# Layer 1's gather table with padded rows and another order of columns

## The chip, the core and the metric

The kernel runs on one core of one Trainium2 chip. The metric is the device time of one execution in microseconds. Several executions are timed, and a profile is taken of one more. The engines named below are TensorE (PE; PEld is its weight load), VectorE (DVE), ScalarE (ACT), GpSimd (POOL) and the queue of SyncE (SP), which issues most transfers. Sixteen DMA engines move the data of all queues.

## The reference

A graph of N = 2708 nodes with 512 features goes through four layers. Each adds its result to its input and applies a layer norm. The adjacency matrix is sparse: about 0.15% of the entries off the diagonal are not zero, and the diagonal is kept.

```python
# layer 0
e1 = adj @ x
x = layernorm(x + (x - e1 * (diag + 1)) @ weight + bias)
# layer 1
type_sum = adj @ x
attn_a = sigmoid(concat(type_sum, x) @ Wa.T + ba);  attn_b = sigmoid(concat(type_sum, x) @ Wb.T + bb)
h = x @ W_sa
scores = (h @ a_left)[:, None] + (h @ a_right)[None, :]
e = where(adj != 0, exp(-leaky_relu(scores, 0.01)), 0)
x_a = (e / (sum(e, 1) + 1e-5)) @ h
x_b = adj @ (x @ W_gcnb) + b_gcnb
x = layernorm(x + sigmoid(attn_a * x_a + attn_b * x_b))
# layer 2: row-normalised incidence of adj times x;  layer 3: tanh(D^-1/2 (adj + I) D^-1/2 x @ W.T + b)
```

## The kernel before

The kernel treats the adjacency as a list of edges. A block is R = 113 destination rows, so there are NB = 24 blocks. Each block's edges off the diagonal are found on the chip in layer 0 and put in EC = 4 chunks of 128 slots; slots without an edge point past the table, and the gather leaves them out. A neighbour sum is then a product on TensorE: a 128 x 113 matrix per chunk, with the edge's value in the column of its destination, times 128 gathered rows. The program also holds a dense version, which does not run on these inputs.

**Layer 0** loads the adjacency block by block, finds the edges with VectorE, gathers rows of x, multiplies with three weight matrices and works in two kinds of pieces: blocks of 113 rows, and windows of 128 rows (`project0`, `residual0`, `norm0`, `next0`, `rest0`). For each window, `next0` and `rest0` compute h = x W_sa, x W_gcnb and four columns of scores and gates and collect them in one row of `st`, a tile from a ring of two. `store0` (L1051) writes that tile to `table[0]` in DRAM. A row before is 2D + 5 = 1029 columns: a one, 512 of h, 512 of x W_gcnb, the right score, the two gate columns, and another one. The first one, summed with the weights e, gives the sum of e; the last, summed with the adjacency values, gives the sum of a row.

**Layer 1** takes its blocks one after the other. `gather1` (L1371, through `gather`, L598) issues four indirect transfers from GpSimd, one per chunk, of whole table rows into one of three tiles `gath`, whose slots are WG = 1032 columns wide; column W1 of the tile, behind what is gathered, is filled with the inverse edge value (`values1`, L1374), so that a sum over it counts edges. `scores1` (L1387, its first instruction at L1390) makes the weights e from the gathered right score. `sums1` (L1402, matmuls at L1407) multiplies the adjacency values with the second half of the row: 256 columns, then 261. `scored_sums1` (L1412, matmuls at L1417) multiplies e with the first half: 257 columns, then 256. `gates1`, `gated1`, `both1`, `stats1` and `norm1` finish the block on VectorE, ScalarE and GpSimd and store it to `table[1]`. The diagonal's contribution doesn't come through the gather: `load_own1` (L634) loads the block's own table rows in order, columns 1 to 2D, to a place that `own_place` (L630) gives: two `shared` tiles and the first weight tile, two blocks in each. `move_rows` (L564) splits every transfer of 113 rows into 112 and 1.

Layers 2 and 3 gather rows of 512 columns from `table[1]` and `table[2]` into the same `gath` tiles, in the same slots.

The order of all instructions on each engine is written out by hand (`tc.manual_schedule()`, L647): engines take them in program order and wait on semaphores. In layer 1 the loop issues the gather of block i+2 while block i is summed, so the gather waits for the sums of block i−1, which read the same tile. On GpSimd the gather stands behind the two small instructions of `stats1` (L1480, L1481) of the block before. On VectorE `scores1` of the next block stands ahead of `stats1` of the last one.

Of the kernel before, what the change touches and what calls it, by code (L numbers as in the profile page):

```python
# [8 lines left out]
FP = mybir.dt.float32  # L9
AF = mybir.ActivationFunctionType  # L10
ALU = mybir.AluOpType
AX = mybir.AxisListType
P = 128
# [5 lines left out]
R = 113  # L19
# [428 lines left out]
def sparse_stack(  # L448
# [29 lines left out]
    nc = tc.nc  # L478
    N, D = x.shape
# [3 lines left out]
    NB = (N + R - 1) // R  # L483
    DB = D // P

    W1 = 2 * D + 5
    WG = 2 * D + 8

    const = ctx.enter_context(tc.tile_pool(name="const", bufs=1))
    dram = ctx.enter_context(tc.tile_pool(name="dram", bufs=1, space=bass.MemoryType.DRAM))  # L490
    big = ctx.enter_context(tc.tile_pool(name="big", bufs=1))
# [3 lines left out]
    def rows(i):  # L495
        return min(R, N - i * R)
# [4 lines left out]
    xr = xr_cols[:, :, :D]  # L501
    table = [dram.tile([N, W1 if k == 0 else D], FP, name=f"table{k}") for k in range(3)]
    deg_d = dram.tile([KB, P], FP, name="deg_d")
# [34 lines left out]
    def column(name, value):  # L538
        t = const.tile([P, NB], FP, name=name)
        nc.gpsimd.memset(t, value)  # L540
        return t

    row_cnt = const.tile([P, NB, 2], FP, name="row_cnt")
    nc.gpsimd.memset(row_cnt, 1.0)
    rowsum, cnt = row_cnt[:, :, 0], row_cnt[:, :, 1]
    adiag = column("adiag", 1.0)
# [17 lines left out]
    def move_rows(r, dst, src):  # L564

        c = r // 16 * 16
        for a, b in ((0, c), (c, r)):
            if a < b:
                nc.sync.dma_start(out=dst(a, b), in_=src(a, b))
# [10 lines left out]
    def times(o, uT, r, w, between=lambda: None):  # L580
        for f in range(DB):
            if f == DB // 2:
                between()
            nc.tensor.matmul(  # L584
                o, lhsT=uT[:, f, :r], rhs=w[:, f, :], start=(f == 0), stop=(f == DB - 1)
            )
# [11 lines left out]
    def gather(g, i, src, n):  # L598
        for c in range(EC):
            nc.gpsimd.indirect_dma_start(  # L600
                out=g[:, c, :n],
                out_offset=None,
                in_=src[:, :],
                in_offset=bass.IndirectOffsetOnAxis(ap=source[:, i, c : c + 1], axis=0),
                bounds_check=last,
                oob_is_err=False,
            )
        return g
# [11 lines left out]
    NGB = 3  # L620
    gath = [big.tile([P, EC, WG], FP, name=f"gath{k}") for k in range(NGB)]
    gflat = [g.rearrange("p c w -> p (c w)") for g in gath]


    shared = [big.tile([P, KB * R], FP, name=f"shared{k}") for k in range(2)]

    w0_sb = big.tile([P, DB, D], FP, name="w0_sb")
    NO = 6

    def own_place(i):  # L630
        t = (*shared, w0_sb.rearrange("p b d -> p (b d)"))[i % NO // 2]
        return t[:, i % 2 * 2 * D :][:, : 2 * D]

    def load_own1(i):  # L634
        r = rows(i)
        own1[i] = own_place(i)
        move_rows(
            r, lambda a, b: own1[i][a:b, :],
            lambda a, b: table[0][i * R + a : i * R + b, 1 : 2 * D + 1],
        )  # L640

    own1 = {}
# [5 lines left out]
    with ExitStack() as phase:  # L648
# [60 lines left out]
        def wrows(w):  # L709
            return min(P, N - w * P)  # L710
# [7 lines left out]
        def to_blocks(w):  # L718

            g, end = w * P, w * P + wrows(w)  # L720
            while g < end:
                i, q = g // R, g % R
                n = min(end, (i + 1) * R) - g
                move_rows(
                    n, lambda a, b: xr_cols[q + a : q + b, i, :],
                    lambda a, b: x1w[w % 2][g - w * P + a : g - w * P + b, :],
                )
                g += n
# [53 lines left out]
        totals = first.tile([P, NB], FP, name="totals")  # L782
        st_ring = [first.tile([P, W1], FP, name=f"st{k}") for k in range(2)]
        for t in st_ring:
            nc.gpsimd.memset(t[:, 0 : W1 : W1 - 1], 1.0)
        nojunk = first.tile([P, KB * R], mybir.dt.uint8, name="nojunk")


# [57 lines left out]
        def negatives(i):  # L846
            nc.scalar.activation(
                nojunk, abuf[i % NA].rearrange("p b i -> p (b i)"), AF.Relu, scale=-1.0,
                accum_out=negs[:, i : i + 1],
            )  # L850
# [175 lines left out]
        def next0(w):  # L1026

            r = wrows(w)
            xT = turned0["x", w]
            st = st_ring[w % 2]  # L1030
            half = (D + 6) // 2
            ends = (0, half, D)
            for k in range(2):
                o = ps_o.tile([P, D], FP, tag="o", name=f"h{k}_{w}")
                times(o[:r, :half], xT, r, w_sa_sb[:, :, k * half : (k + 1) * half])
                nc.scalar.copy(
                    st[:r, 1 + ends[k] : 1 + ends[k + 1]], o[:r, : ends[k + 1] - ends[k]]
                )
            col = o[:r, half - 6 : half]
            nc.scalar.copy(x1w[w % 2][:r, D:], col)  # L1040
            nc.scalar.copy(st[:r, 2 * D + 1 : 2 * D + 4], col[:, 1:4])
            to_blocks(w)
            st0[w] = st
# [112 lines left out]
        negatives(2)  # L1156
        for a, b in ((0, EC * D), (EC * D + 4 * D + 12, EC * WG)):
            nc.scalar.memzero(gflat[1][:, a:b])
# [148 lines left out]
    ediag = const.tile([P, NB], FP, name="ediag")  # L1307
# [20 lines left out]
    for g, (c0, _) in enumerate(SEGS):  # L1328
        at = slice(8 * g, 8 * g + 8)
# [12 lines left out]

    H = D // 2
    e_at = (slice(0, 1 + H), slice(1 + H, 1 + D))
    s_at = (slice(1 + D, 1 + D + H), slice(1 + D + H, W1 + 1))
    SR = 2 * D + 1

    def halves(t, r):  # L1350
        return t[:r, :].rearrange("p (k d) -> p k d", k=2)
# [3 lines left out]
    edge_s, edge_e, sum_s, sum_e, vb1, gate1, v1 = ({} for _ in range(7))  # L1355
# [15 lines left out]
    def gather1(i):  # L1371
        gather(gath[i % NGB], i, table[0], W1)

    def values1(i, chunks):  # L1374

        if i not in edge_s:
            edge_s[i] = spool.tile([P, EC, R], FP, tag="s", name=f"s1_{i}", bufs=3)
            nc.scalar.copy(gath[i % NGB][:, :, W1], inverse[:, i, :])
        for c in chunks:
# [32 lines left out]
    def scored_sums1(i):  # L1412
        g, e, r = gath[i % NGB], edge_e.pop(i), rows(i)
        sum_e[i] = ps_1e.tile([P, 2, D], FP, tag="e1", name=f"l1e{i}")
        for k, at in enumerate(e_at):
            for c in range(EC):
                nc.tensor.matmul(  # L1417
                    sum_e[i][:r, k, k : k + at.stop - at.start], lhsT=e[:, c, :r],
                    rhs=g[:, c, at], start=(c == 0), stop=(c == EC - 1),
                )  # L1420

    def gates1(i):

        r = rows(i)

        gate1[i] = small.tile([P, 2], FP, tag="gate", name=f"gate{i}")
        nc.vector.tensor_add(
            gate1[i][:r, :], sum_s[i][:r, 1, H + 1 : H + 3], gates[:r, i, :]
        )
        nc.scalar.activation(gate1[i][:r, :], gate1[i][:r, :], AF.Tanh, scale=0.5)  # L1430
        nc.scalar.copy(row_cnt[:r, i, :], sum_s[i][:r, 1, H + 3 : H + 5])

    def gated1(i):

        r = rows(i)
        vb = vb1[i] = spool.tile([P, D], FP, tag="vb", name=f"l1b{i}")
        nc.vector.scalar_tensor_tensor(  # L1437
            halves(vb, r), halves(own1[i][:, D:], r), adiag[:r, i : i + 1],
            sum_s.pop(i)[:r, :, :H], op0=ALU.mult, op1=ALU.add,
        )  # L1440
        nc.vector.tensor_add(vb[:r, :], vb[:r, :], bg_bc[:r, :])
        gate = gate1[i]
        nc.vector.tensor_scalar(
            gate[:r, :], gate[:r, :], 0.5, 0.5, op0=ALU.mult, op1=ALU.add
        )
        nc.scalar.activation(vb[:r, :], vb[:r, :], AF.Copy, scale=gate[:r, 1:2])

    def both1(i):

        r, agg = rows(i), sum_e.pop(i)  # L1450
        rec = small.tile([P, 1], FP, tag="rec", name=f"rec{i}")
        nc.vector.scalar_tensor_tensor(
            rec[:r, :], agg[:r, 0, 0:1], 1e-5, ediag[:r, i : i + 1], op0=ALU.add, op1=ALU.add
        )
        nc.vector.reciprocal(rec[:r, :], rec[:r, :])
        nc.vector.tensor_mul(rec[:r, :], rec[:r, :], gate1.pop(i)[:r, 0:1])
        va = work.tile([P, D], FP, tag="u", name=f"l1a{i}")
        nc.vector.scalar_tensor_tensor(
            halves(va, r), halves(own1.pop(i)[:, :D], r), ediag[:r, i : i + 1],
            agg[:r, :, 1 : H + 1], op0=ALU.mult, op1=ALU.add,  # L1460
        )
        v = work.tile([P, D], FP, tag="v", name=f"l1v{i}")
        nc.vector.scalar_tensor_tensor(
            v[:r, :], va[:r, :], rec[:r, :], vb1.pop(i)[:r, :], op0=ALU.mult, op1=ALU.add
        )

        nc.scalar.activation(v[:r, :], v[:r, :], AF.Tanh, scale=0.5)
        v1[i] = v
# [126 lines left out]
    for i in range(NB):  # L1595
# [3 lines left out]
        if i > 0:  # L1599
            both1(i - 1)  # L1600
# [272 lines left out]
```

## Time and profile before

| | |
|---|---|
| runs, median (lowest to highest) of 3 | 988.39 us (983.14 to 991.57) |
| profiled execution | 972.5 us |
| its span, first to last instruction | 970.3 us |
| granted TensorE clock, mean | 0.967 |
| bytes moved by DMA | 201.69 MB in 133516 packets, mean 208 GB/s |
| packets under 512 B | 82457 |
| gathers from the tables | 288 issues; issue to landing 3.1, 4.4, 9.6 us (least, median, most) |
| stages in the span | layer 0 to about 410 us, layer 1 to about 625, layer 2 to about 773, layer 3 to the end |

In the lines of the profile an instruction is named by its line in the source, its engine, and output <- inputs, with buffer numbers left out. `gath<-table,source` is a gather from any of the tables; `shared<-table` and `w_sb<-table` are own rows. An idle time is put down to the instruction whose end released it. A table of stretches gives each engine's busy time, then the granted clock, the mean busy share of the 16 DMA engines, and the rate at which they moved data.

### The profile page before, as it was taken

The page shows a single profiled execution, that of the slowest core. Times are in us where ns is not written, and L with a number is a line of the kernel's source. Part 1 is how long each engine was busy: PE and PEld are TensorE (multiplying, and loading weights), DVE is VectorE, ACT ScalarE, POOL GpSimd, SP SyncE. Part 2 cuts the span into 40 slices and gives each one's busy share as a digit, 9 for nine tenths or more (in the row PEclk, how much of TensorE's full clock was granted, in tenths as well). Part 3 has the DMA queues.
Part 4 walks back from the last instruction along what each step waited for, and adds up shares of the span by engine and source line. Part 5 has one row for each costly group of instructions (what it writes and reads, how often), then busy time and mean ns, then how long its engine had stood idle before and what let it go on. Part 6 is the DMA issues. An engine that isn't in the chain of part 4 may idle for free.

```text
span 970.3 us, 11188 instructions
## 1 busy us (share of the span) xinstructions
PE 890.4 (92%) x2957; PEld 492.3 (51%) x2957; DVE 686.6 (71%) x1807; ACT 528.0 (54%) x1221; POOL 466.6 (48%) x536
## 2 busy tenths in 40 slices
PE   6789999999999999988898899888898989999994
PEld 2446556556565555456676677533333334444441
DVE  7787899878898853068887879777777526556543
ACT  5676667867677753357776777434455312222222
POOL 3223232423133220066666667367777478767640
PEclk8889999999999999989999999999999999999998
DMA  9987786987888444388999998257777556655531
GB/s 242 317 206 199 209 244 185 281 221 220 215 234 236 138 133 144 110 283 274 299 297 310 305 299 279 97 161 220 215 227 213 142 164 182 177 155 173 163 108 32
DMA packets 133516, 201.69 MB, mean 208 GB/s; under 512 B 82457, under 2 KB 82503, under 8 KB 133446
## 3 DMA queue, kind: packets, MB, share of 16 engines
q0 software_dynamic: 36864, 111.73, 39.1%
q1 hardware_dynamic: 96581, 89.18, 32.1%
q8 instruction: 25, 0.41, 0.2%
q14 instruction: 46, 0.37, 0.1%
HBM read 181.83 MB, written 27.80 MB: 216 GB/s over the span
## 4 chain that ended last, share of the span: by engine, by line
PE 58%; DMA 19%; DVE 8%; issue 5%; POOL 5%; SPq 2%; ACT 2%; POOLq 0%; DVEq 0%; ACTq 0%
DMA gath<-table,source 16%; PE o_l L584 15%; PE l3a L613 9%; PE hb L584 7%; PE h L584 7%; PE l0a L613 6%; POOL gath L600 4%; PE l2a L613 3%; PE l1s L1407 2%; PE fetched L915 2%; PE unread L1537 2%; SPq L677 2%; DMA gath<-in_x_dram 1%; PE l1e L1417 1%; PE tr_l L1066 1%
## 5 line engine op out<-in xcount | busy, mean ns | idle before, releaser
L600 POOL DMA_INDIRECT gath<-table,source x288 | 314.4, 1092 | 158.2 <-issue 62.8
L600 POOL DMA_INDIRECT gath<-in_x_dram,source x96 | 97.2, 1013 | 224.8 <-issue 189.4
L1407 PE MATMUL l1s<-gath,s 128*113 128x256 f32 (+3 forms) x384 | 98.3, 412 | 21.1 <-DVE l1b L1437 20.6
L613 PE MATMUL l2a<-gath,s_left 128*113 128x512 f32 (+1 forms) x192 | 96.8, 619 | 16.4 <-DMA gath<-table,source 16.2
L1407 PEld LDWEIGHTS l1s<-gath,s 128*113 128x113 f32 (+1 forms) x384 | 71.5, 191 | 48.2 <-DVE l1b L1437 28.1
L613 PE MATMUL l3a<-gath,s 128*113 128x512 f32 (+1 forms) x192 | 88.3, 602 | 3.1 <-DMA gath<-table,source 3.1
L613 PE MATMUL l0a<-gath,s 128*113 128x512 f32 (+1 forms) x192 | 87.3, 595 | 0.5 <-DMA gath<-in_x_dram,source 0.5
L584 PE MATMUL o_l<-shared,uT_l 128*113 128x512 f32 (+1 forms) x192 | 86.5, 593 | 0.7 <-ACT uT_l L577 0.7
L1417 PE MATMUL l1e<-gath,e 128*113 128x257 f32 (+3 forms) x384 | 87.0, 379 | 0.0
L584 PE MATMUL hb<-w_gc_sb,uT_x 128*128 128x512 f32 (+1 forms) x176 | 83.3, 601 | 0.0
L584 PE MATMUL o_l<-w_sb,uw 128*128 128x512 f32 (+1 forms) x176 | 81.4, 606 | 0.2
L584 PE MATMUL h<-w_sa_sb,uT_x 128*128 128x259 f32 (+1 forms) x352 | 80.8, 382 | 0.0
L1417 PEld LDWEIGHTS l1e<-gath,e 128*113 128x113 f32 (+1 forms) x384 | 68.0, 177 | 15.3 <-DVE e L1400 0.2
L584 PEld LDWEIGHTS h<-w_sa_sb,uT_x 128*128 128x128 f32 (+1 forms) x352 | 64.8, 185 | 19.8 <-issue 6.1
L1792 ACT ACTIVATE y<-l3v,mv_l 113x512 f32<-113x512 f32 (+1 forms) x24 | 19.5, 813 | 87.4 <-DVE mv_l L1788 80.6
L613 PEld LDWEIGHTS l2a<-gath,s_left 128*113 128x113 f32 (+1 forms) x192 | 29.6, 179 | 73.1 <-DMA gath<-table,source 56.2
L584 PEld LDWEIGHTS o_l<-shared,uT_l 128*113 128x113 f32 (+1 forms) x192 | 33.9, 178 | 48.9 <-issue 47.3
L613 PEld LDWEIGHTS l0a<-gath,s 128*113 128x113 f32 (+1 forms) x192 | 33.3, 177 | 41.1 <-issue 36.2
L613 PEld LDWEIGHTS l3a<-gath,s 128*113 128x113 f32 (+1 forms) x192 | 32.6, 180 | 41.6 <-issue 38.3
L1294 DVE TENSOR_SCALAR s<-niota_r,nrow,edges 128x113 f32<-128x113 f32 x192 | 51.4, 345 | 0.0
L1766 DVE SCALAR_TENSOR_TENSOR l3v<-o_l,d_inv,b_bc 113x512 f32<-113x512 f32 (+1 forms) x25 | 18.1, 728 | 46.8 <-PE o_l L584 46.7
L862 DVE FIND_INDEX8 where_all<-rec_all,shared 128x8 uint32<-128x678 f32 (+1 forms) x64 | 51.2, 800 | 0.0
(244 smaller groups left out, 1573.9 us busy)
## 6 DMA issues: line engine op xcount, KB each, us to landing
shared<-in_adj_dram SPq DMA_DIRECT2D x14, 1186.5 KB
table<-st SPq DMA_DIRECT2D x21, 514.5 KB
gath<-in_adj_dram SPq DMA_DIRECT2D x7, 1186.5 KB
shared<-table SPq DMA_DIRECT2D x16, 448.0 KB
gath<-in_x_dram SPq DMA_DIRECT2D x21, 256.0 KB
xi<-in_x_dram SPq DMA_DIRECT2D x23, 224.0 KB
table<-xr SPq DMA_DIRECT2D x23, 224.0 KB
table<-y SPq DMA_DIRECT2D x23, 224.0 KB
```

The source lines that it names most:

```text
L584: nc.tensor.matmul(o, lhsT=uT[:, f, :r], rhs=w[:, f, :], start=(f == 0), stop=(f == DB - 1))
L600: nc.gpsimd.indirect_dma_start(out=g[:, c, :n], out_offset=None, in_=src[:, :], in_offset=bass.IndirectOffsetOnAxis(ap=source[:, i, c : c ...
L613: nc.tensor.matmul(agg[:r, :], lhsT=s[:, c, :r], rhs=g[:, c, off : off + D], start=(c == 0), stop=(c == EC - 1),)
L677: nc.sync.dma_start(out=a[:TAIL, NF, :r], in_=adjT[NF * P :, at])
L862: nc.vector.max_index(out=where_all[:, i, g * 8 : (g + 1) * 8], in_max=top, in_values=seg)
L915: nc.tensor.matmul(t["fetched"][:, c, : 3 * NS], lhsT=t["q"][:, c * P : (c + 1) * P], rhs=rec_all[:, i].rearrange("p k s -> p (k s)"), sta ...
L1294: nc.vector.tensor_scalar(s[:, c, :], niota_r, nrow[:, i, c : c + 1], edges[:, i, c, 1:2], op0=ALU.is_equal, op1=ALU.mult,)
L1407: nc.tensor.matmul(sum_s[i][:r, k, : at.stop - at.start], lhsT=s[:, c, :r], rhs=g[:, c, at], start=(c == 0), stop=(c == EC - 1),)
L1417: nc.tensor.matmul(sum_e[i][:r, k, k : k + at.stop - at.start], lhsT=e[:, c, :r], rhs=g[:, c, at], start=(c == 0), stop=(c == EC - 1),)
L1537: nc.tensor.matmul(o[:, :cols], lhsT=ident, rhs=bg_bc[:, :cols], start=True, stop=True)
L1766: nc.vector.scalar_tensor_tensor(v[:r, at], o[:r, at], d_inv[:r, i : i + 1], b3_bc[:r, at], op0=ALU.mult, op1=ALU.add,)
L1792: nc.scalar.activation(y[:r, :], v[:r, :], AF.Identity, bias=mv[:r, 3:4], scale=mv[:r, 2:3])
```

## The change

Table rows become W1 = 1040 columns, 2D + 5 rounded up to 16, with zeros in the 11 columns added. A slot of `gath` becomes W1 + 4 = 1044 columns. The one for the sum of e moves from the start of the row to the place behind h, so that h starts the row and x W_gcnb, the scores, the gates and the last one keep their columns. Own rows are loaded as the first 1025 columns, from the start of the row, and take 1025 columns in their places; the first weight tile grows by two columns for it. The matmuls of `scored_sums1` take 256 and then 257 columns; the second half in `sums1` runs on to the inverse edge values behind the padding, so it takes 272 columns where it took 261. `gates1` picks the row sum and the count out of it with a step of 12. The transfers, and the order of instructions, stay as they are; one more memset per `st` tile is added. (What the diff writes as a new width and order of columns is all of it; layer 0's order of work is the same in both kernels.)

```diff
-    W1 = 2 * D + 5
-    WG = 2 * D + 8
+    W1 = (2 * D + 5 + 15) // 16 * 16
+    WG = W1 + 4
...
-    w0_sb = big.tile([P, DB, D], FP, name="w0_sb")
+    w0_own = big.tile([P, 4 * D + 2], FP, name="w0_sb")
+    w0_sb = w0_own[:, : DB * D].rearrange("p (b d) -> p b d", d=D)
     NO = 6
 
     def own_place(i):
-        t = (*shared, w0_sb.rearrange("p b d -> p (b d)"))[i % NO // 2]
-        return t[:, i % 2 * 2 * D :][:, : 2 * D]
+        t = (*shared, w0_own)[i % NO // 2]
+        return t[:, i % 2 * (2 * D + 1) :][:, : 2 * D + 1]
 
     def load_own1(i):
...
-            lambda a, b: table[0][i * R + a : i * R + b, 1 : 2 * D + 1],
+            lambda a, b: table[0][i * R + a : i * R + b, : 2 * D + 1],
...
         for t in st_ring:
-            nc.gpsimd.memset(t[:, 0 : W1 : W1 - 1], 1.0)
+            nc.gpsimd.memset(t[:, 2 * D + 5 :], 0.0)
+            nc.gpsimd.memset(t[:, D : 2 * D + 5 : D + 4], 1.0)
...
                 nc.scalar.copy(
-                    st[:r, 1 + ends[k] : 1 + ends[k + 1]], o[:r, : ends[k + 1] - ends[k]]
+                    st[:r, ends[k] : ends[k + 1]], o[:r, : ends[k + 1] - ends[k]]
                 )
...
-    e_at = (slice(0, 1 + H), slice(1 + H, 1 + D))
+    e_at = (slice(0, H), slice(H, 1 + D))
     s_at = (slice(1 + D, 1 + D + H), slice(1 + D + H, W1 + 1))
...
-                    sum_e[i][:r, k, k : k + at.stop - at.start], lhsT=e[:, c, :r],
+                    sum_e[i][:r, k, : at.stop - at.start], lhsT=e[:, c, :r],
...
-        nc.scalar.copy(row_cnt[:r, i, :], sum_s[i][:r, 1, H + 3 : H + 5])
+        nc.scalar.copy(row_cnt[:r, i, :], sum_s[i][:r, 1, H + 3 : H + 4 + W1 - 2 * D - 4 : W1 - 2 * D - 4])
...
-            halves(vb, r), halves(own1[i][:, D:], r), adiag[:r, i : i + 1],
+            halves(vb, r), halves(own1[i][:, D + 1 :], r), adiag[:r, i : i + 1],
...
-            rec[:r, :], agg[:r, 0, 0:1], 1e-5, ediag[:r, i : i + 1], op0=ALU.add, op1=ALU.add
+            rec[:r, :], agg[:r, 1, H : H + 1], 1e-5, ediag[:r, i : i + 1], op0=ALU.add, op1=ALU.add
...
-            agg[:r, :, 1 : H + 1], op0=ALU.mult, op1=ALU.add,
+            agg[:r, :, :H], op0=ALU.mult, op1=ALU.add,
```

## The prediction

> **What bounds the kernel now.** I read the page first, for the engines and the chain of work that ended last.
>
> ```profile
> span 970.3 us, 11188 instructions
> PE 890.4 (92%) x2957; PEld 492.3 (51%) x2957; DVE 686.6 (71%) x1807; ACT 528.0 (54%) x1221; POOL 466.6 (48%) x536
> ...
> PE 58%; DMA 19%; DVE 8%; issue 5%; POOL 5%; SPq 2%; ACT 2%; POOLq 0%; DVEq 0%; ACTq 0%
> DMA gath<-table,source 16%; PE o_l L584 15%; PE l3a L613 9%; PE hb L584 7%; PE h L584 7%; PE l0a L613 6%; POOL gath L600 4%; PE l2a L613 3%; PE l1s L1407 2%; PE fetched L915 2%; PE unread L1537 2%; SPq L677 2%; DMA gath<-in_x_dram 1%; PE l1e L1417 1%; PE tr_l L1066 1%
> ```
>
> TensorE carries most of the chain, but its largest single term is a transfer: gathers from the tables, 16% of the span. The changed table feeds layer 1 (about 423 to 616 us), so next come busy times by stretch. Columns: PE, PEld, DVE, ACT, POOL busy us, granted clock, DMA share, GB/s.
>
> ```profile
> 423.00:440.00 17.00, 15.01 (x62) 10.88 (x61) 10.89 (x25) 9.02 (x26) 10.44 (x12) 0.93 0.92 326
> 440.00:585.00 145.00, 128.10 (x544) 99.66 (x544) 119.74 (x306) 101.95 (x255) 94.97 (x102) 0.95 0.96 299
> 589.00:616.00 27.00, 25.24 (x114) 19.43 (x112) 24.43 (x62) 19.38 (x49) 16.05 (x18) 1.00 0.67 228
> 640.00:770.00 130.00, 115.26 (x262) 41.91 (x262) 95.60 (x263) 62.43 (x115) 95.60 (x93) 0.99 0.73 209
> 785.00:950.00 165.00, 164.17 (x454) 72.27 (x455) 90.51 (x217) 42.11 (x67) 111.06 (x133) 1.00 0.55 157
> ```
>
> From 440 to 585 us the DMA engines are 96% busy; nothing else is. From 589 us the last gathers are in and PE is 93% busy. Which wait ends last shows in VectorE's order of time, at its first instruction on a gathered block (`scores1`, L1390):
>
> ```profile
> 503.24 0.63 DVE L1390 TENSOR_TENSOR e<-gath,s_left 128x452 f32<-128x452 f32 x1
> 512.61 0.63 DVE L1390 TENSOR_TENSOR e<-gath,s_left 128x452 f32<-128x452 f32 x1 [1.66 <-DMA gath<-table,source]
> ...
> 596.87 0.62 DVE L1390 TENSOR_TENSOR e<-gath,s_left 128x452 f32<-128x452 f32 x1
> 604.49 0.62 DVE L1390 TENSOR_TENSOR e<-gath,s_left 128x452 f32<-128x452 f32 x1
> ```
>
> Without a wait a block takes 7.62 us (604.49 − 596.87); while gathers run, blocks take 7.6 and 9.4 us in turn, and the long one has a wait on the gather. Between 435.92 and 589.25 us, 18 blocks take 8.52 us each. So a perfect DMA could return at most 18 × (8.52 − 7.62) = 16.2 us here; the waits named DMA sum to 14.4 us (1.32, 0.87, 1.42, 0.48, 1.38, 1.66, 1.91, 1.43, 0.33, 2.04, 1.35, 0.22).
>
> [...] The trace can test this on the adjacency loads, whose pieces are unaligned at both ends:
>
> ```profile
> DMA packets 7936, 3.52 MB, mean 282 GB/s; under 512 B 7936, under 2 KB 7936, under 8 KB 7936
> ```
>
> That is 2.5 to 15 us: 12.5 us × 16 engines / 7936 = 25.2 ns a piece. [...] what the trace shows of speed is the 25.2 ns above, with pieces that land off any 32 B grid.
>
> **The change part by part.** The order of instructions on every engine is unchanged except for two more memsets on GpSimd; no DMA is moved past another, no wait is added.
>
> *Gather source, 4116 B at pitch 4116 to 4160 B at pitch 4160 (64 B aligned).* About 452 rows per block. [...] By bytes it is a loss: 44 × 452 = 19.9 KB per block at 299 GB/s = 0.067 us, × 18 blocks = 1.2 us if all of it is on the path. I take the middle of 0 and 1.2: **+0.6 us**. [...] The adjacency loads bound it: [...] misalignment, and all else, is at most about 9 ns a piece. Per block each engine handles 28 gathered rows and 7 own rows; 35 × 9 ns × 18 = 5.7 us. Gain between 0 and 5.7 us; value taken 0[...].
>
> *Own rows, 4096 B from 4 B past a row start to 4100 B from the start.* [...] nothing, and counted in the 35 above. The 113th row goes alone: [...] taken as 0.
>
> *Gather destination.* Compiled addresses: all slots of `gath` began on a 32 B boundary at pitch 4128; at pitch 4176 slots 1 and 3 begin 16 B past one. [...] Bound from both sides: no gain, because no slot gets a better start; cost at most the same 9 ns on half the rows: 14 per engine and block × 9 ns × 18 = 2.3 us in layer 1, and in layer 2 (22 blocks, about 0.6 on the path, as PE is 89% busy there) 1.7 us; layer 3 is hidden by PE, busy 164.17 of 165 us. Taken 0, range 0 to 4.
>
> *Matmuls.* The shape rows of TensorE:
>
> ```profile
> L1407 PE MATMUL l1s<-gath,s 128*113 128x256 f32 x184 | 51.3, 425 | 20.8 <-DVE l1b L1437 20.4 <-POOL mv_l L1481 0.3
> L1407 PE MATMUL l1s<-gath,s 128*113 128x261 f32 x184 | 47.2, 402 | 0.0
> ```
>
> The 261 columns become 272. A block's 16 passes of `l1s` take 3.74 us for 8 × 517 = 4136 columns, 0.90 ns each; 88 more are 0.08 us. Until 585 us the waits on gathers hide this (cover gone: 20 × 0.08 = 1.6 us). In the last four blocks it is on the path: **+0.3 us**. `l1e` swaps 257+256 for 256+257: nothing.
>
> *Nothing, with cover.* Stores of the table: 44 × 2708 B = 119 KB, 0.4 us at 299 GB/s, spread over layer 0, where DMA is 67 to 78% busy and PE 252 of 255 us. Memsets of 11 columns: about 0.2 us at 3.8 us, covered by GpSimd's 0.73 us of waiting for the adjacency. ACT's clears: 3 × 48 more elements at 0.9 ns = 0.13 us; the first lies in a 2.15 us wait, the others could show 0.1 us. The strided `row_cnt` copy still moves two elements.
>
> **Sum:** +0.6 + 0.3 = +0.9 us on the profiled execution, 972.5 (span 970.3 plus 2.2 around it) to 973.4. The median of the runs is 988.39, 1.6% above that execution; I carry the 0.9 over: **989.3 us**. Its own range, from the bounds: −5.7 + 0.3 to +1.2 + 1.6 + 4.0 + 0.8 (clears, memsets, stores uncovered), 983 to 996.
>
> **Rivals.** *Faster: [...]* Random 4 KB rows are not adjacency pieces; if each misaligned read also costs memory time, 35 rows × t × 18 blocks = 630 t. From t = 16 ns the gain passes 1%; that is 8% of the 0.21 us an engine spends per row (26.00 MB on the gather queue in 70.4% of 16 engines' time from 440 to 560 us). It saturates when the DMA waits are gone: −14.4 + 1.5 of matmul then uncovered, about −13; halfway between threshold and end: 977 us. For: DMA is at 96%, and 299 GB/s is below the best slices of 423 to 440 us. Against: those slices reach 428 GB/s with the same unaligned rows.
>
> *Slower: half of all gathered rows now land off the 32 B grid.* Place: layers 1 and 2. Price: 14 rows per engine and block × t × (18 + 13) = 434 t; beyond t = 23 ns it costs 10 us and decides; at 28 ns, 12 us and **1000 us**. For: before, every row started on the grid. Against: the adjacency pieces land off it at 25 ns in all.
>
> *It does not do what it says:* DMA limits layer 1 through the number of rows and the two gathers in flight[...]; then only TensorE's 0.3 us remain: 988.7, inside the forecast.
>
> **Numbers.** Forecast 0.55, faster 0.27, slower 0.18. A difference of 1% (about 10 us) is about what a measurement of this kernel can tell from no change. The range 977 to 999 leaves out about half of each rival, 2 in 10.
>
> **What would show it.** Packets under 512 B fall by 24 × 16 = 384 to about 82070; moved bytes rise to 202.3 MB; `l1s` shows 128x272; L1390 keeps its alternation of 7.6 and 9.4 us and its 14 us of waits. Rate per engine in the gathers of 440 to 585 us rising by over 8%, and the waits vanishing, would be the first rival; longer waits of `l2a` on gathers in layer 2 would be the second. What I would have most wrong is a memory cost that 452 B pieces don't show.

## The result, and the profile after

Twelve executions of each kernel give 986.02 us in the median for the changed kernel (981.04 to 991.32) and 990.14 us for the one before (983.14 to 992.35). The recorded ratio is 0.9982, with a 95% interval of 0.996 to 1.0004: no difference. (The quotient of the two medians is lower, 0.9958; in a later series, below, it is 0.9996, with a recorded ratio of 0.9993.) The prediction was 989.3 us, "no change".

The profiled execution of the changed kernel seems to say otherwise: 985.9 us, span 984.2, where the profile before had a span of 970.3. So this section asks two things: whether the predicted terms are there, and what the 14 us between the two profiles are. First the page of the kernel after: its span, its engines, its DMA packets, and the chain of work that ended last by engine.

```profile
span 984.2 us, 11190 instructions
PE 891.9 (91%) x2957; PEld 495.6 (50%) x2957; DVE 686.6 (70%) x1807; ACT 527.7 (54%) x1221; POOL 468.8 (48%) x538
...
DMA packets 133515, 202.29 MB, mean 206 GB/s; under 512 B 82456, under 2 KB 82502, under 8 KB 133445
...
PE 64%; DMA 12%; DVE 7%; issue 5%; POOL 4%; ACT 2%; another core or an unknown queue 2%; SPq 2%; POOLq 0%; DVEq 0%; ACTq 0%
```

The two added instructions are there (POOL x538, before x536), and so is the padding: 202.29 MB, before 201.69. Packets under 512 B are 82456 where they were 82457; the prediction wanted 384 fewer. The busy times of the engines are those of before within 3.3 us. New in the chain is "another core or an unknown queue", 2%: the chain stands at an instruction that waited for something the profile cannot name.

Next the busy times by stretch of the kernel after; the columns are those of the table before (PE, PEld, DVE, ACT, POOL busy us, granted clock, DMA share, GB/s).

```profile
440.00:585.00 145.00, 125.10 (x546) 96.24 (x545) 120.22 (x307) 102.43 (x255) 96.96 (x104) 0.99 0.97 305
...
640.00:770.00 130.00, 108.26 (x244) 42.49 (x244) 87.17 (x236) 55.77 (x106) 94.99 (x90) 0.93 0.69 200
785.00:950.00 165.00, 158.72 (x424) 69.15 (x425) 84.56 (x206) 39.14 (x62) 114.39 (x134) 0.97 0.56 161
```

Layer 1 (440 to 585 us) is as before: DMA 97% busy (96%), 305 GB/s (299). Layers 2 and 3 are where PE does less in the same time: 108.26 of 130 us where it was 115.26, and 158.72 of 165 where it was 164.17. GpSimd, which issues the gathers, is busy for 94.99 us in the first (before 95.60) and 114.39 in the second (before 111.06).

VectorE's order of time in layer 1, at the first instruction of `scores1` (now L1394), shows the same alternation and the same kind of wait:

```profile
432.29 0.62 DVE L1394 TENSOR_TENSOR e<-gath,s_left 128x452 f32<-128x452 f32 x1
...
534.59 0.63 DVE L1394 TENSOR_TENSOR e<-gath,s_left 128x452 f32<-128x452 f32 x1 [1.75 <-DMA gath<-table,source]
542.33 0.63 DVE L1394 TENSOR_TENSOR e<-gath,s_left 128x452 f32<-128x452 f32 x1
551.99 0.63 DVE L1394 TENSOR_TENSOR e<-gath,s_left 128x452 f32<-128x452 f32 x1 [1.95 <-DMA gath<-table,source]
...
585.47 0.63 DVE L1394 TENSOR_TENSOR e<-gath,s_left 128x452 f32<-128x452 f32 x1 [0.46 <-DMA gath<-table,source]
600.95 0.62 DVE L1394 TENSOR_TENSOR e<-gath,s_left 128x452 f32<-128x452 f32 x1
608.53 0.62 DVE L1394 TENSOR_TENSOR e<-gath,s_left 128x452 f32<-128x452 f32 x1
```

Blocks 7.7 and 9.7 us apart (542.33 − 534.59, 551.99 − 542.33), the long one ending with a wait on a gather; 18 blocks from 432.29 to 585.47 us, so 153.18 us, where it was 153.33; waits at this line of 14.16 us in all, 12.47 of them put down to the gathers and one of 1.69 to nothing that the profile names; before, 14.4 were put down to the gathers. The last starts, without gathers to wait for, are 7.63 and 7.58 us apart; before, the same two distances are 7.62 and 7.59.

The chain of the kernel after, in order of time, from layer 2 on: start, length, what it was spent on.

```profile
668.38 5.93 another core or an unknown queue
...
704.91 2.44 another core or an unknown queue
...
731.91 5.67 another core or an unknown queue
...
766.47 2.92 another core or an unknown queue
...
805.66 4.97 another core or an unknown queue
```

These are 21.9 us, and the profile before has none. The account of the two spans: layer 0 ends earlier (the first instruction of `scores1` starts at 420.94 us, before 424.54: −3.6), the 18 blocks −0.15, layer 2 from the first to the last of its 24 normalisations (`l2v<-l2a` on VectorE) 134.6 us where it was 123.7: +10.9, and what is then missing of +13.9, with the 4.97 us at 805.66 in it, +6.8. The experiments must tell whether these waits belong to the change.

### The profile page after: what moved, and what is told of

Its sections match the earlier page's. It is cut to its first block, busy times and chain, and to the rows that moved or that the text cites. A ratio compares the mean times of both kernels' runs of the same rounds, so it can differ in the third digit from the quotient of the medians.

```text
span 984.2 us, 11190 instructions
## 1 busy us (share of the span) xinstructions
PE 891.9 (91%) x2957; PEld 495.6 (50%) x2957; DVE 686.6 (70%) x1807; ACT 527.7 (54%) x1221; POOL 468.8 (48%) x538
## 2 busy tenths in 40 slices
DMA packets 133515, 202.29 MB, mean 206 GB/s; under 512 B 82456, under 2 KB 82502, under 8 KB 133445
## 4 chain that ended last, share of the span: by engine, by line
PE 64%; DMA 12%; DVE 7%; issue 5%; POOL 4%; ACT 2%; another core or an unknown queue 2%; SPq 2%; POOLq 0%; DVEq 0%; ACTq 0%
PE o_l L585 15%; DMA gath<-table,source 9%; PE l3a L614 9%; PE l2a L614 8%; PE hb L585 8%; PE h L585 7%; PE l0a L614 7%; POOL gath L601 3%; PE unread L1541 2%; PE fetched L918 2%; SPq L679 1%; PE l1s L1411 1%; PE tr_l L576 1%; PE tr_l L1069 1%
## 5 line engine op out<-in xcount | busy, mean ns | idle before, releaser
L1411 PE MATMUL l1s<-gath,s 128*113 128x256 f32 (+3 forms) x384 | 95.9, 404 | 22.2 <-DVE l1b L1441 21.9
L1411 PEld LDWEIGHTS l1s<-gath,s 128*113 128x113 f32 (+1 forms) x384 | 68.8, 184 | 49.6 <-DVE l1b L1441 30.2
L614 PE MATMUL l3a<-gath,s 128*113 128x512 f32 (+1 forms) x192 | 90.5, 616 | 2.8 <-DMA gath<-table,source 2.8
L1421 PE MATMUL l1e<-gath,e 128*113 128x256 f32 (+3 forms) x384 | 87.0, 379 | 0.0
L1421 PEld LDWEIGHTS l1e<-gath,e 128*113 128x113 f32 (+1 forms) x384 | 68.2, 178 | 15.4
L1541 PE MATMUL unread<-bg_bc,ident 128*128 128x512 f32 x80 | 44.2, 669 | 21.3 <-remote 17.1
L614 PEld LDWEIGHTS l2a<-gath,s_left 128*113 128x113 f32 (+1 forms) x192 | 33.9, 190 | 57.5 <-issue 38.7
```

The lines of the kernel that those rows point to most:

```text
L614: nc.tensor.matmul(agg[:r, :], lhsT=s[:, c, :r], rhs=g[:, c, off : off + D], start=(c == 0), stop=(c == EC - 1),)
L1411: nc.tensor.matmul(sum_s[i][:r, k, : at.stop - at.start], lhsT=s[:, c, :r], rhs=g[:, c, at], start=(c == 0), stop=(c == EC - 1),)
L1421: nc.tensor.matmul(sum_e[i][:r, k, : at.stop - at.start], lhsT=e[:, c, :r], rhs=g[:, c, at], start=(c == 0), stop=(c == EC - 1),)
L1541: nc.tensor.matmul(o[:, :cols], lhsT=ident, rhs=bg_bc[:, :cols], start=True, stop=True)
```

## The experiments

The theory is that of the prediction: layer 1's blocks wait for DMA throughput, the padding costs little more than its bytes, and alignment decides nothing. Against it stand three rivals: the start of an unaligned source row costs time of its own, 16 ns a row or more (the faster one, theory B below); destinations off the 32 B grid cost time (the slower one); and gathers limited by the number of rows and by having two blocks under way, not by the bytes that they move (theory C). The measure is the stretch of 18 blocks in layer 1, from the third to the twenty-first start of `scores1`'s first instruction, read in each profile; the whole time goes by medians, against runs of the kernel before on the same chip. There were three series: the first without own rows, the wide pitch and one size of slots; the second the wide pitch again, the order of columns alone, and the kernel before; the third the changed kernel and both sizes of slots.

### Layer 1 without its own rows

```diff
         own1[i] = own_place(i)
-        move_rows(
-            r, lambda a, b: own1[i][a:b, :],
-            lambda a, b: table[0][i * R + a : i * R + b, 1 : 2 * D + 1],
-        )
```

This is the kernel before, without layer 1's own-row loads, a fifth of what it moves per block (113 of about 565 rows); the gathers, their number and their order stay. The diagonal's part of layer 1 is computed from whatever lies in those tiles.

> The kernel before, with the loads of own rows in layer 1 left out (the diagonal's part of layer 1 is then computed from stale data; every other instruction stays). Measure: the 18 blocks of layer 1 between the third and the twenty-first start of scores1, 153.3 us in the kernel before. Theory A, layer 1 waits on what 16 DMA engines can move: per block 0.46 of 2.55 MB go, 8.52 x 0.82 = 7.0 us is below the 7.62 us that a block takes without waits, so the stretch falls to 137 to 140 us, the waits of scores1 on gathers to under 3 us, and the whole kernel is 13 to 16 us faster. Theory C, layer 1 waits on the latency of two gathers in flight and not on throughput: the stretch falls by less than 5 us.

Measured: 972.35 us against 990.05, ratio 0.983 (0.9785 to 0.9876). VectorE's order of time in this kernel, the same instruction (here L1386), and the stretch of 440 to 585 us:

```profile
503.57 0.62 DVE L1386 TENSOR_TENSOR e<-gath,s_left 128x452 f32<-128x452 f32 x1
511.19 0.62 DVE L1386 TENSOR_TENSOR e<-gath,s_left 128x452 f32<-128x452 f32 x1
518.81 0.62 DVE L1386 TENSOR_TENSOR e<-gath,s_left 128x452 f32<-128x452 f32 x1
526.47 0.63 DVE L1386 TENSOR_TENSOR e<-gath,s_left 128x452 f32<-128x452 f32 x1
```

```profile
440.00:585.00 145.00, 136.51 (x608) 105.97 (x608) 132.46 (x341) 113.22 (x286) 111.47 (x114) 1.00 0.84 278
```

Every block takes 7.6 us, no start has a wait, and PE does 136.51 us of work in the 145 where it did 128.10. The 18 blocks take 137.91 us instead of 153.33: 15.4 of the at most 16.2 us that the prediction read off. So layer 1 waits for what the DMA engines carry in all, and having only two gathers under way, which is so here too, doesn't hold it back: that half of the third rival falls. The other half, rows against bytes, isn't decided by this run, which takes both away; the next section has more on it.

The same run answers for the 113th row. The page's packets:

```profile
DMA packets 130386, 190.58 MB, mean 197 GB/s; under 512 B 82036, under 2 KB 82082, under 8 KB 130317
```

The copy of the kernel before (run below) has 133445 packets under 8 KB and 82456 under 512 B. So the own rows of 24 blocks were 133445 − 130317 = 3128 packets, of which 82456 − 82036 = 420 are small. The other 2708 are exactly one packet a row, the single rows too. In the packet records of the two traces the 2708 are all the packets of 4096 B on that queue, and the 420 are 4 B each. That the small ones go with the transfers is read from their number alone: it fits 16 beside 112 rows, 1 beside a single row, and 16 and 13 beside the last block's 109 rows, which are split into 96 and 13: 23 × (16 + 1) + 16 + 13 = 420. A store of 113 rows in layer 2 of the kernel after has the same count, 113 packets of 2048 B and 17 of 4 B from 694 to 696 us. A single row of 4096 B travels whole, as one packet.

### Where rows start: a wide pitch, from and off a 256 B boundary

The changed kernel with rows of 4352 B (17 × 256), 59 unused columns ahead of the data that are gathered too. In one kernel every row starts at a 256 B boundary, counted from the start of the table; in the other, every row starts 252 B past one, with the same bytes gathered to the same places. (A constant of layer 3 lies in another tile, to make room.) The stores and own rows leave the unused columns out and start off the boundary in both, 236 and 232 B past one. The core of the edit (S = 0 or 63; the offset of the gather is in the second kernel alone):

```diff
-    W1 = (2 * D + 5 + 15) // 16 * 16
+    K, S = 59, 0
+    W1 = K + 2 * D + 5
...
+    rows1 = table[0].rearrange("n w -> (n w)")[S : S + N * W1].rearrange("(n w) -> n w", w=W1)
...
                 in_offset=bass.IndirectOffsetOnAxis(ap=source[:, i, c : c + 1], axis=0),
+                element_offset=off,
...
-        gather(gath[i % NGB], i, table[0], W1)
+        gather(gath[i % NGB], i, table[0], W1, S)
...
-    e_at = (slice(0, H), slice(H, 1 + D))
+    e_at = (slice(K, K + H), slice(K + H, K + 1 + D))
```

The unused columns are zeroed at the start of layer 0, in pieces of 236 B; these pieces, too, start on or off the boundary.

> The changed kernel with a pitch of 1088 columns (4352 B, a multiple of 256 B), all 1088 gathered, 59 unused columns ahead of the data, so that every gathered row starts on a 256 B boundary: [...] 192 B more. The third bias row moves to a shared tile to make room, and the unused columns are zeroed early in layer 0, which may cost a few us there; the layer-1 stretch (153.2 us in the changed kernel) is what counts. [...] A by bytes: 192 x 452 B at 299 GB/s x 18 = +5.2 us, 158 us. Theory B, [...] the stretch is below 153 us in spite of the bytes. Theory C: 153 us.

> The same as the run before it, but every gathered row starts 252 B past a 256 B boundary (63 columns further on; same bytes, same rows, same places in the tiles): [...] This is the cost of an unaligned start by itself. [...] Theory B: at least 16 ns a row, +8 us or more. By bytes, and by theory C: no difference (under 1 us).

Measured: 999.77 us, ratio 1.0095 (1.0063 to 1.0127), from the boundary; 1001.57 us, ratio 1.0126 (1.0098 to 1.0154), from 252 B past it. Both were run again on another chip:

> The wide rows that start on a 256 B boundary once more, for a second profile. The first had 157.9 us in the layer-1 stretch, 4.7 over the changed kernel, as the bytes alone would have it (158); but the same rows started 252 B past the boundary had 154.0. If the 3.9 us between them are of the start: 157.5 to 158.5 again. If they are spread of one profile against another: anywhere between 154 and 158.

> The wide rows started 252 B past a boundary once more. [...] if they cost nothing, the two agree within the spread; if rows on a boundary are slower for another reason, 154 again against 158.

Measured: 983.89 us, ratio 1.0117 (1.0077 to 1.0157), and 987.3 us, ratio 1.0153 (1.0109 to 1.0198). The 18 blocks of the first pair, first the kernel from the boundary, then the one off it:

```profile
443.32 0.62 DVE L1404 TENSOR_TENSOR e<-gath,s_left 128x452 f32<-128x452 f32 x1
...
601.21 0.63 DVE L1404 TENSOR_TENSOR e<-gath,s_left 128x452 f32<-128x452 f32 x1 [2.87 <-DMA gath<-table,source]
```

```profile
446.48 0.62 DVE L1405 TENSOR_TENSOR e<-gath,s_left 128x452 f32<-128x452 f32 x1
...
600.47 0.66 DVE L1405 TENSOR_TENSOR e<-gath,s_left 128x452 f32<-128x452 f32 x1 [1.17 <-DMA gath<-table,source]
```

157.89 us from the boundary, 153.99 off it; in the repeats, between the same instructions, 157.00 and 155.37. At the rival's 16 ns a row, 28 rows per engine and block and 18 blocks, the kernel off the boundary would be an estimate of 8.1 us longer. It was 2.8 us shorter on average. So the start off the boundary costs nothing here, and the faster rival falls: there was no cost of unaligned rows for the change to remove.

The packet records of the traces say the same row by row (gather queue, 440 to 560 us). The commonest time of one row is 160 ns at 4116 B, 161 ns at 4160 B, and 168 ns at 4352 B, from the boundary and off it alike, in both pairs; the rival's 16 ns would be a tenth of that. In the run without own rows, where rows start anywhere, 71% of them take exactly 160 ns, so this doesn't hang on where the table itself begins. The time of a row grows with its bytes, about 26 B per ns in all three sizes, and not with its start. That also speaks against a price per row that doesn't depend on bytes. (Other rows take longer than the commonest time; the mean is 208 to 216 ns in every kernel with own rows.)

What of the difference in the whole time is not in layer 1? The first product with the layer's weights (`o_l<-w_sb,uw`), in order of time on PE, in the kernel before, then the wide one from the boundary, then the one off it:

```profile
54.12 4.96 PE L584 MATMUL o_l<-w_sb,uw 128*128 128x512 f32 x8
```

```profile
62.38 5.70 PE L587 MATMUL o_l<-w_sb,uw 128*128 128x512 f32 x8
```

```profile
66.57 4.65 PE L587 MATMUL o_l<-w_sb,uw 128*128 128x512 f32 x8
```

Layer 0 starts 8.3 us late with the zeroing from the boundary and 12.5 us late with it off the boundary (repeats: 62.89 and 67.65). From there to the end of the last such product of layer 0 the two kernels take the same: 340.6 and 339.8 us from the boundary, 339.6 and 340.7 off it. So the wide kernels' loss is mostly the price of my own zeroing, and 2708 short pieces written off the boundary cost about 4 us more than on it; by the packet records a piece took 27 and 23 ns on average in the two kernels from the boundary, 54 and 57 ns off it. The whole times of this pair must not be read as a verdict on row starts.

### Destination slots

The changed kernel with slots of 1048 columns, which all begin on a 32 B boundary again, and with 1045, where the four slots begin 0, 20, 8 and 28 B past one, counted from the start of the tile.

```diff
-    WG = W1 + 4
+    WG = 1048
```

```diff
-    WG = W1 + 4
+    WG = 1045
```

> The changed kernel with slots of 1048 instead of 1044 columns (4192 B), so that all four slots of a gather tile begin on a 32 B boundary again; nothing else. Theory A: destination starts cost nothing that counts; layer-1 stretch 153 us, layer 2 blocks unchanged, the total within 0.4%. The slower rival, that slots off the grid cost time: up to 2.3 us less in layer 1 and up to 1.7 us less in layer 2.

Measured in the first series: 986.52 us, ratio 0.997 (0.9952 to 0.9988). That was a small gain where the changed kernel itself had 0.9982, so both slots and the kernel as it is were run in one series, in which they share their runs of the kernel before:

> The changed kernel once more, beside the kernel before on whatever chip this is. Revised theory A: layer 1 is bound by the bytes that 16 DMA engines move, and where a row starts counts for nothing; the change adds 20 KB per block, at most +1.2 us, and the two profiles of each kernel differ by more than that. So: layer-1 stretch 153 to 155 us, total within 0.4% of before, in either direction. If the 0.2% that the first comparison showed in its favour is real, it shows again: a ratio of 0.997 to 0.999 with an interval below 1. No unnamed waits in layers 2 and 3 if this is the chip of the run before this one, several if it is the first.

> The changed kernel with slots of 1048 columns, all on the 32 B grid, once more; its first ratio was 0.997 (0.9952 to 0.9988). Theory A: as the changed kernel, within 0.2%. If the grid of the slots is worth something: at least 0.2% better than the changed kernel.

> The changed kernel with slots of 1045 columns (4180 B): three of the four slots of each gather tile begin 20, 8 or 28 B past a 32 B boundary, in layers 1 to 3. Theory A: nothing, total within 0.2% of the changed kernel, layer-1 stretch 153 to 155 us. The slower rival: half again as many rows off the grid as in the changed kernel, and none of them on 16 B; up to 3.5 us more in layer 1 and 2.5 us more in layer 2 at 9 ns a row, more if the rival's 23 ns hold.

| kernel | median us | ratio to before (95%) | 18 blocks, us | layer 2, us |
|---|---|---|---|---|
| before, same series | 971.99 | | | |
| the changed kernel again | 971.62 | 0.9993 (0.9975 to 1.0011) | 154.22 | 123.5 |
| slots of 1048, on the grid | 972.41 | 1.0000 (0.9981 to 1.0019) | 156.06 | 123.8 |
| slots of 1045, off the grid | 973.12 | 1.0005 (0.9982 to 1.0028) | 154.92 | 123.6 |

"Layer 2" is the stretch of its 24 normalisations, as above. No order by the grid appears in either column, and the commonest time of a gathered row is 161 ns in all three kernels: the slower rival falls. The small gain of the first series isn't repeated. The slots on the grid give 153.16 us for the 18 blocks in the first series and 156.06 in the third, so one kernel's own spread is up to 2.9 us, and a term of 0.6 us can't be seen in one profile.

### The order of columns without the padding, and the kernel before again

```diff
-    W1 = (2 * D + 5 + 15) // 16 * 16
-    WG = W1 + 4
+    W1 = 2 * D + 5
+    WG = 2 * D + 8
...
-            nc.gpsimd.memset(t[:, 2 * D + 5 :], 0.0)
```

> The new order of columns and own rows from the start of the row, with the old pitch of 1029 columns and slots of 1032: the order alone, without padding or alignment. Theory A: nothing moves; layer-1 stretch 153.3 us within 0.5, total within 0.4% of before. If own rows in one piece from the row's start are what helps: up to 1 us less in the stretch. If alignment of rows is what the change pays with or for: same as before here.

> The kernel before once more, for a second profile. Its first profiled execution (972.5 us) was 1.6% under the median of its runs, while that of the changed kernel was 985.9; the changed one shows three to five waits of 2 to 6 us in layers 2 and 3 in which TensorE is released by nothing that the profile names. Theory A: these waits have nothing to do with the change; this profile shows them too, in the same stages, some 15 to 20 us in the chain, and a time near 988; the layer-1 stretch is 153.3 us within 0.5. If the waits come from the change (slots off the 32 B grid in layers 2 and 3), this profile has none. Layer 0 up to the first start of scores1: 424.5 us in the first profile, 420.9 in the changed kernel; if the aligned stores are what differs, 424 again, else anything between 420 and 426.

Measured beside the kernel before at 970.55 us: the order alone 971.48, ratio 1.0009 (0.9994 to 1.0023), 18 blocks 153.38 us; the copy of the kernel before 970.2, ratio 0.9992 (0.9972 to 1.0012), 18 blocks 154.69 us. The order of columns, with own rows loaded from the start of the row, is worth nothing either. The copy also settles layer 0: its `scores1` first starts at 420.78 us, the changed kernel's at 420.94 and the first profile's of before at 424.54. The 3.6 us by which layer 0 seemed shorter are spread. The copy's 18 blocks are 1.4 us over the first profile, more than the 0.5 expected.

### The unnamed waits

They are in the first profile of the changed kernel, five times, and in every profile of the first series. The kernel without own rows, otherwise the kernel before, has four. Its chain:

```profile
655.02 5.92 another core or an unknown queue
...
698.72 3.85 another core or an unknown queue
...
730.89 4.91 another core or an unknown queue
...
790.51 5.00 another core or an unknown queue
```

They are in no profile of the two later series, of either kernel. There the changed kernel runs at 971.62 us, and the kernel before at 970.55 and 971.99 us, instead of 990. Two expectations fail here. The copy of the kernel before was to show the waits if the change has nothing to do with them; it shows none, which taken alone would speak for the change. And the changed kernel was to have them again on the chip of the first series; it has none. Chip and kernel don't decide: the first and the third series ran on the same chip, the kernel without own rows lacks the change and has them, and the changed kernel runs without them. (The kernel before itself was profiled twice, both times without them.) Layer 2, from 640 to 770 us, in the copy of the kernel before, which has none of them:

```profile
640.00:770.00 130.00, 114.13 (x258) 41.35 (x257) 93.01 (x254) 61.58 (x114) 97.55 (x92) 0.98 0.69 205
```

PE has 114.13 us of work there, close to the 115.26 of the first profile of before. The 24 normalisations of layer 2 take 123.5 to 126.8 us in the profiles without these waits and 131.3 to 134.6 in those with them. So these waits aren't made by the change, and the 14 us between the first two profiles aren't its effect: they come and go with the executions, and the kernels keep level whether both run at 990 us (ratio 0.9982) or at 972 (0.9993). What they are stays open. The waits of the kernel after say where they sit (who waited, for what; sum, number and longest in us):

```profile
PE unread L1541 <- remote: 17.1, 4, 5.9
...
DVE l2v L1694 <- remote: 12.3, 2, 7.3
```

In the one at 668.38 us PE, ScalarE and VectorE stand for 5 to 6 us, and GpSimd goes on issuing gathers. The packets of the instruction queues fall beside the five waits and not within them (the nearest in 702 to 704 and 710 to 712 us, around the wait from 704.91 to 707.35), so the profile doesn't connect the two.

## Why the prediction was right, and where it wasn't

*What bounds the kernel.* Right, and shown: without the own rows the blocks run at 7.6 us and 15.4 of the 16.2 us come back.

*The gather's source, +0.6 us, the middle of 0 and 1.2 us by bytes.* The forecast of no visible change holds. Its lower end, 0, was the author's estimate, in which the aligned start gives back what the padding costs. That reason failed: rows 252 B off the boundary were 2.8 us shorter in the stretch than rows on it, so there was nothing to give back. That the value held all the same was luck. Bytes fare better. One ns more a row, as the packet records have it, is an estimate of 0.5 us for 28 rows and 18 blocks; three profiles with rows of 4116 B average 153.8 us (153.33, 154.69, 153.38) and five with 4160 B average 154.3 (153.18, 153.16, 154.22, 156.06, 154.92). That is +0.5 us beside a spread of up to 2.9, so the +0.6 is allowed, not shown, in the stretch. For 192 B more, bytes would be 5.2 us at the rate of the whole core (192 × 452 / 299 GB/s × 18), or 3.5 by the 7 ns between the commonest times; the two wide kernels give +3.1 and +0.4 us over the average of those five. Why the wide rows on the boundary took longer than those off it isn't known; their difference is about the spread of a single kernel.

*The unaligned start at up to 5.7 us, taken 0; the destination at up to 4 us, taken 0.* The 9 ns a piece behind both bounds were the author's estimate. From what the traces show, 452 B at the rate of a gathered row (4116 B in 160 ns, 25.7 B per ns) would be 17.6 of the 25.2 ns of an adjacency piece, which leaves an estimate of 7.6 ns, or 4.8 and 3.3 us. Both values hold, by the wide pair and by the slots, as far as a spread of 2.9 us in the stretch can tell; the packet times show neither cost.

*Own rows: 384 packets under 512 B fewer.* This step failed. The prediction took it that a single row travels in several pieces, and in fewer of them after the change; no run had shown that. The packets show one a row in the kernel before, 2708 of 4096 B, and in the kernel after, 2708 of 4100 B. It cost nothing because the step had been taken as 0.

*Matmuls, +0.3 us in the last four blocks.* The size was right, the path wrong. These are the 16 passes of `l1s` in one of the last blocks, in order of time on TensorE, before and then after; the profile merges both shapes under the name of the first:

```profile
600.87 3.74 PE L1407 MATMUL l1s<-gath,s 128*113 128x256 f32 x16 [0.42 <-DVE l1b L1437]
```

```profile
604.95 3.82 PE L1411 MATMUL l1s<-gath,s 128*113 128x256 f32 x16 [0.34 <-DVE l1b L1441]
```

They take 0.08 us longer, as priced. But TensorE waits ahead of them until VectorE has finished `l1b`, and that wait is 0.08 us shorter: 0.42 and 0.34. So the blocks stay 7.6 us apart (7.62 and 7.59 before, 7.63 and 7.58 after), and the term is nothing. The prediction took "93% busy" for being on the path and left this wait out, though its own line of `l1s` shows 20.4 us of it in all.

*Stores, memsets, clears at nothing.* Nothing is seen of them: layer 0 ends as early as in the copy of the kernel before.

*The sum.* Its +0.9 us is too small for the whole times to show: their intervals leave −4.0 to +0.4 us in the first comparison and −2.4 to +1.1 in the repeat. What these do exclude is a gain or a loss of 10 us, that is, the two rivals.

*The profiled execution and the median.* The prediction noted 1.6% between them and carried its sum over as a difference, which is what kept it right. The series without the unnamed waits run at the level of that first profile; that the waits are the whole of the 1.6% is the likeliest reading, but a timed execution leaves no trace to show it.

*The rivals.* Faster: fell, since alignment has no price here to give back. Slower: fell, since slots 0, 20, 8 and 28 B off the grid run like slots on it. "DMA limits by the number of rows and two gathers in flight": the gathers in flight fell with the run without own rows; against the number of rows speak the packet times, 160 to 168 ns, which go with the bytes. Its time, 988.7, couldn't have told it from the forecast in any case.

## What to carry to other kernels

Where a stretch is shown to wait for DMA throughput, look for bytes and for whole transfers to take away: a fifth of the rows and their bytes gone was worth 15 us, while the alignment of rows of 4 KB, at the source or the destination, was worth nothing that could be measured. A price read off short pieces may say nothing of long rows: the 25.2 ns of a 452 B adjacency piece left room for one on the start, and rows of 4352 B took 168 ns from either start. So it needs a test on the size that it is used for. An engine that is 93% busy may still have slack at one place in each block (here a wait of 0.42 us that became 0.34), so look for a wait just ahead of an instruction before its added length is counted. And before a difference between two profiles is put down to a change, ask whether a copy of the kernel before would show it as well: here 14 us in the spans, and 3.6 us in layer 0, were not the change's.

## What the runs showed of the hardware that was not expected

- Rows of 4352 B gathered from starts 252 B past a 256 B boundary took no longer than rows from the boundary: 154.0 and 155.4 us for 18 blocks against 157.9 and 157.0. The commonest time of one such row was 168 ns for both; it was 160 ns for rows of 4116 B, wherever they began, and 161 ns for rows of 4160 B, whether or not their slots in the tile began on a 32 B boundary.
- Short pieces do feel it: zeroing 236 B in each of 2708 rows, with rows 252 B off the boundary instead of on it, delayed layer 0's first product by another 4.2 to 4.8 us (62.38 and 62.89 to 66.57 and 67.65); a piece took 54 and 57 ns on average instead of 27 and 23.
- Single-row transfers of 4 KB went as one packet each: 2708 packets of 4096 B for 2708 own rows in the kernel before, 2708 of 4100 B in the kernel after.
- The same kernel ran at 990 us in one series and at 972 in another on the same chip, with waits of up to 5.9 us on TensorE, 9.8 on ScalarE and 7.3 on VectorE in the first profile of the changed kernel, taken in the slower series, whose releaser no record names.
